# Moving head-norm, value and key-projection steps between the slots of the first two cycles of a fused two-block transformer kernel

## The chip, the cores and the metric

The kernel runs on one core of one Trainium2 chip. The metric is the device time of one execution, in microseconds (us). A core has five engines that take part here: TensorE (PE, matrix multiplication, with a separate record PEld for loading weights), VectorE (DVE), ScalarE (ACT), GpSimd (POOL) and SyncE (SP, which only issues transfers). Each has its own instruction queue and they wait for one another through semaphores.

## The reference, cut to what matters

Two transformer blocks run one after the other over `x` of shape (8, 512, 256): batch 8, 512 tokens, width 256. All data are float32. The first block ("block 0") is the one that the change touches:

```python
mod = silu(c) @ adaln_w.T + adaln_b            # nine rows of 256 per batch element
h = ln(x) * (1 + scale_sa) + shift_sa
q = ln(heads(h)) * qn_w + qn_b                 # 16 heads of 16 columns, each head normed
k = ln(heads(h)) * kn_w + kn_b
x = x + gate_sa * softmax(q k^T / 4) heads(h)  # self-attention, values are h itself
h = ln(x) * (1 + scale_ca) + shift_ca
kv = brain @ cond_w.T + cond_b                 # 64 context tokens of width 192
x = x + gate_ca * (attention(h wq, kv wk, kv wv) @ ca_out_w.T + ca_out_b)
h = ln(x) * (1 + scale_ff) + shift_ff
x = x + gate_ff * ((silu(h w1) * (h w3)) @ w2)
```

The second block has self-attention with 16 heads of 64 columns and rotary position factors, cross-attention to the layer-normed context with rotated keys (`ctx_n @ ca_wk`, computed once for all batch elements), and a GELU feed-forward part.

## The kernel before, in words

Block 0 is one long list of slots. A cycle is 18 slots (`CYCLE = H + 2`), and cycle b holds the 16 score blocks of batch element b: four groups g of four heads, four key tiles kt each, at slots 0 to 17 without 11 and 13 (`X0`, `X1`). In slots 11 and 13 of cycle b + 1 stand the two cross-attention score blocks of element b; in cycle 0 they are empty. Feed-forward of element b runs in cycle b + 2. "Slot n" below counts from the start of the kernel, so cycle 1 is slots 18 to 35.

A score block multiplies four heads at once (PE, tile `ps_S`, L118, 16 rows of each head against 512 query columns), ACT takes the exponential of two halves of 1024 columns (L596, tile `p`), and a value block multiplies `p` by `h` into `ps_O`. There are two `ps_S` tiles and one score block fills both, so the next score block waits for the exponentials of the one before.

All other work is hung on slots by `at(slot, function)`. `run_blocks` walks the slots: in the first 18 it issues the scores of slot i, the values of slot i - 1 and then what `at` hung on slot i; from there on it takes slots in pairs. The order of issue is the order of each engine's queue: the section is recorded under a manual schedule, so nothing is reordered later, and functions on one slot come in the order of their `at` calls. Entries in the list `later` are hung on after everything else.

The steps concerned:

- Head norm of the next element (`batch1`, L640 to L662). After the layer norm and modulation of `h`, the 16 heads are normed in two halves c = 0 and c = 1: `head_centre` (DVE L548 to L550: mean, subtract, into `z`), `head_square` (ACT L554), `head_var` (DVE L560, L561) and `head_scale` (POOL: the power -1/2 at L567 and the product at L568). For element 0 the half c = 0 is split again by parity; `first_modulated` (DVE L535, L536) modulates `h` out of the PSUM tile `first_mod`.
- `queries_keys(g)`: four PE transposes of `z` (L576), then q on ACT (L579) and k on DVE (L580). Group g uses half c = g // 2. For element 1, g = 0 stands in slot 16 and g = 2 in slot 20.
- `group_end` (ACT copy L609) and `group_back(g)`: PE transposes (L616), DVE L623 to L625, then POOL's gating L627 and the addition to `x` L628.
- Set-up of cross-attention: `values0(t)`, t = 0 to 3 (two PE matmuls of 256 columns, four DVE additions L380 into `vb0`), `modulation1` (L391), `modulation1_columns` (PE L396, DVE L397), and the layer-normed context for block 1, turned by `context1(k)` (PE L415, DVE L416).
- Keys of block 1: `keys1(p)`, p = 0 to 7 (two PE matmuls of 512 columns with `w_ck`, DVE L847 and L850 twice, POOL L851) and `store_keys1(p)` (a transfer issued on POOL's queue, L873). `open_cross` at slot 18 closes the set-up pool, and SP then issues the load of `w_ck` into its place (L264).

PSUM tiles for everything else come from `bank_x`: every third is the bank `ps_D`, the others are the two `ps_X` banks. A bank is written again only after its last reader is done.

## Time and profile before

| what | value |
|---|---|
| median of 3 runs (lowest, highest) | 2392.32 us (2385.81, 2396.17) |
| the profiled execution, its own time | 2395.5 us |
| span of that execution on the core | 2393.4 us |
| mean granted TensorE clock | 0.994 |
| PE busy | 2369.5 us, 99% |
| DVE, ACT, POOL busy | 1140.9, 887.8, 960.2 us |

The profiled execution's own time is 2.1 us above its span, which is what lies around the first and last instruction, and 3.2 us above the median. The profile gives times from the span's start. Each group of instructions has its line in the kernel, its engine, the tile it writes and those it reads; `x8` behind four matmuls of float32 is the number of machine instructions. PE's ends are modelled: a score block that stands with 2.04 us instead of 1.14 us has its second half held up, not more work.

The first two cycles reach from 17 us to about 171 us of the span. PE is idle for 3.35 us of the first 60 us, 6.77 us of the second 60 us (53.23 us busy) and 0.84 us of the third. In the second 60 us the granted clock averages 0.83.

### The profile page before, as it was taken

The numbers are of one execution on the slowest core, as the hardware profiler recorded it, in microseconds if no ns is written. First come the engines' busy times: TensorE is split into PE (matmuls) and PEld (weight loads), VectorE is DVE, ScalarE is ACT, GpSimd is POOL, SyncE is SP. The second block draws the span as 40 slices with busy tenths as digits, with TensorE's granted clock in tenths as the row PEclk, the third lists the DMA queues.
The fourth block names the chain that finished last, engine by engine and source line by source line (L and its number), as shares of the span: only waits on it lengthen the run. The fifth ranks groups of instructions, "written<-read, shape, count | busy, mean of one in ns | idle before, by whom it ended". The sixth has DMA issues, their size and how long they took to land.

```text
span 2393.4 us, 28547 instructions
## 1 busy us (share of the span) xinstructions
PE 2369.5 (99%) x10964; PEld 1156.6 (48%) x10964; DVE 1140.9 (48%) x2115; ACT 887.8 (37%) x1118; POOL 960.2 (40%) x588
## 2 busy tenths in 40 slices
PE   9899999999999999999999999999999999999998
PEld 4333544534545633444444444444345566667665
DVE  4464534535335445545455454545444766651110
ACT  4566545555552134333333333333332222221221
POOL 4463323233201037555555555555543545541110
PEclk9899999999999999999999999999999999999999
DMA  5121000000002000000000000000113222210000
GB/s 185 28 88 35 16 13 11 17 16 8 11 14 92 1 1 24 19 19 19 19 19 19 19 19 19 19 19 19 37 56 105 71 68 69 65 57 30 18 23 19
DMA packets 84897, 84.07 MB, mean 35 GB/s; under 512 B 42656, under 2 KB 59792, under 8 KB 84752
## 3 DMA queue, kind: packets, MB, share of 16 engines
q1 hardware_dynamic: 83208, 78.99, 10.6%
q8 instruction: 88, 1.44, 0.2%
q0 software_dynamic: 640, 2.10, 0.2%
q10 hardware_dynamic: 904, 1.07, 0.1%
q14 instruction: 57, 0.47, 0.1%
HBM read 72.09 MB, written 10.04 MB: 34 GB/s over the span
## 4 chain that ended last, share of the span: by engine, by line
PE 94%; DVE 2%; POOL 1%; issue 1%; DMA 1%; ACT 1%; SPq 0%; POOLq 0%; DVEq 0%; ACTq 0%
PE ps_X L118 39%; PE ps_S L118 24%; PE ps_D L118 15%; PE ps_O L118 14%; PE ps_X L429 1%; POOL var L567 1%; DMA rb<-rec 1%; PE ps_X L616 0%; PE ps_X L576 0%; DVE t L850 0%; DMA rec<-rec 0%; PE ps_D L576 0%; PE ps_D L429 0%; PE ps_D L616 0%; ACT p L596 0%
## 5 line engine op out<-in xcount | busy, mean ns | idle before, releaser
L118 PE MATMUL ps_S<-q,k 32*128 32x512 f32 (+1 forms) x3072 | 421.3, 628 | 5.5 <-ACT p L596 3.4
L1027 ACT ACTIVATE p<-ps_S 128x1024 f32<-128x1024 f32 x256 | 248.4, 1021 | 449.4 <-PE ps_S L118 449.1
L596 ACT ACTIVATE p<-ps_S 128x1024 f32<-128x1024 f32 x256 | 248.2, 1022 | 201.3 <-PE ps_S L118 200.4
L118 PEld LDWEIGHTS ps_S<-q,k 32*128 32x128 f32 (+1 forms) x3072 | 143.0, 185 | 231.9 <-issue 162.5
L1046 DVE TENSOR_TENSOR sm<-sm,p 128x1024 f32<-128x1024 f32 x128 | 252.4, 2030 | 0.1
L1009 POOL TENSOR_TENSOR q<-t 128x512 f32<-128x512 f32 x32 | 59.7, 1866 | 331.3 <-DVE t L1007 290.2
L1006 DVE TENSOR_TENSOR t<-ps_X,rope_c 128x512 f32<-128x512 f32 x126 | 86.9, 689 | 213.0 <-PE ps_X L118 213.0
L184 POOL TENSOR_TENSOR rstd<-rstd,mhalf 128x4 f32<-128x4 f32 x49 | 50.1, 1023 | 331.8 <-DVE rstd L183 330.4
L851 POOL TENSOR_TENSOR q<-t,t 128x512 f32<-128x512 f32 x72 | 94.9, 1318 | 159.2 <-DVE t L850 159.2
L567 POOL TENSOR_TENSOR var<-var,mhalf 128x32 f32<-128x32 f32 (+1 forms) x17 | 87.3, 5137 | 159.0 <-DVE var L561 158.9
L1042 POOL TENSOR_TENSOR sm<-p 128x1024 f32<-128x1024 f32 x64 | 150.0, 2370 | 1.9 <-ACT p L1027 1.9
L118 PE MATMUL ps_X<-hT,w 128*128 128x512 f32 x328 | 150.4, 597 | 0.0
L1092 POOL TENSOR_TENSOR oT<-oT,rb 128x512 f32<-128x512 f32 x63 | 126.9, 2032 | 28.8 <-DMA rb<-rec_d 28.8
L118 PE MATMUL ps_O<-p,v 128*64 128x512 f32 x512 | 134.9, 605 | 0.0
L118 PE MATMUL ps_O<-p,h 128*32 128x512 f32 x1024 | 131.6, 618 | 0.6 <-ACT p L596 0.6
L118 PE MATMUL ps_D<-p,v 128*64 128x512 f32 x512 | 131.6, 592 | 0.0
L118 PE MATMUL ps_X<-w_sa_wv,hT 128*128 128x512 f32 x256 | 118.0, 604 | 0.0
L118 PE MATMUL ps_X<-hT,w_sa_wq 128*128 128x512 f32 x256 | 115.9, 595 | 0.0
L118 PE MATMUL ps_X<-w_sa_wo,oT 128*128 128x256 f32 x512 | 113.9, 381 | 0.6 <-DVE t L1007 0.5
L118 PE MATMUL ps_X<-hT,w_sa_wk 128*128 128x512 f32 x248 | 113.2, 599 | 0.0
L466 DVE TENSOR_TENSOR x<-ps_X,x 128x512 f32<-128x512 f32 x27 | 18.7, 691 | 195.6 <-PE ps_X L118 195.6
L118 PE MATMUL ps_S<-hT,w_ff_w 128*128 128x512 f32 x256 | 111.3, 593 | 0.0
(285 smaller groups left out, 3622.0 us busy)
## 6 DMA issues: line engine op xcount, KB each, us to landing
rb<-rec SPq DMA_DIRECT2D x128, 128.0 KB
rb<-rec_d SPq DMA_DIRECT2D x124, 128.0 KB
rb<-rec SPq DMA_DIRECT2D x16, 256.0 KB
out_dram<-x SPq DMA_DIRECT2D x15, 256.0 KB
x<-in_x_dram SPq DMA_DIRECT2D x7, 512.0 KB
gate<-modd SPq DMA_DIRECT2D x24, 128.0 KB
k_d<-q POOLq DMA_DIRECT2D x8, 256.0 KB, 2.4
v_d<-v SPq DMA_DIRECT2D x8, 256.0 KB
```

The source lines that it names most:

```text
L118: nc.tensor.matmul(o, lhsT, rhs, start=start, stop=stop)
L184: nc.gpsimd.tensor_tensor(r[:, :n], r[:, :n], mhalf[:, :n], ALU.pow)
L429: nc.tensor.transpose(ps[:, t * P : (t + 1) * P], z[:, t, k * P : (k + 1) * P], ident)
L567: nc.gpsimd.tensor_tensor(var, var, half, ALU.pow)
L596: nc.scalar.activation(pr[u], pss[u], AF.Exp, scale=HD0 ** -0.5)
L851: nc.gpsimd.tensor_tensor(dst, t1, t2, ALU.add)
L1006: nc.vector.tensor_tensor(c, ps, rope_c, ALU.mult)
L1009: nc.gpsimd.tensor_tensor(r[0], ec, os, ALU.subtract)
L1027: nc.scalar.activation(pr, pss[u], AF.Exp, scale=HD1 ** -0.5)
L1042: nc.gpsimd.tensor_tensor(sm, s["p", g, 0, u], s["p", g, 1, u], ALU.add)
L1046: nc.vector.tensor_tensor(s["sm", g, u], s["sm", g, u], s["p", g, t, u], ALU.add)
L1092: eng.tensor_tensor(o, o, s["rb", g, u], ALU.mult)
```

## The change

Four things move between slots; no instruction is added or taken away.

- Element 1's head norm: its two halves ran together in slots 12 to 14. Now half 0 has its `head_scale` in slot 13 instead of 14, in front of `group_back(2)`'s gating of slot 14 on POOL's queue, and half 1 runs in slots 15 to 17.
- `values0(0..3)` stood in slots 10, 11, 14 and 15 and stands in 14, 15, 16 and 17.
- `keys1(p)` stood in slots 22, 23, 25, 27, 28, 30, 32 and 33 and stands in 20, 22, 24, ... 34. `store_keys1(p)` stood in slots 25, 26, 28, 30, 31, 33, 35 and 36 and stands in 23, 25, 27, 29, 31, 33, 35 and 36.
- Element 0's `first_modulated(1)` stays in slot 2 but goes behind `queries_keys(1)` of that slot, through `later`, whose definition moves up for it.

```diff
@@ batch1
                         for k, par, fns in ((0, 1, (first_modulated, head_centre)),
-                                            (1, 1, (head_square, head_var, head_scale)), (2, None, (first_modulated,)),
+                                            (1, 1, (head_square, head_var, head_scale)),
                                             (3, None, (head_centre,)), (4, None, (head_square, head_var, head_scale))):
                             for fn in fns:
                                 at(k, lambda fn=fn, par=par: fn(0 if par else 1, par))
                         at(5, lambda: spread(s["gate"], b, G_SA, D))
+                        later.append((at, 2, lambda: first_modulated(1)))
                     else:
 
                         for m, k in enumerate((-11, -10, -9) if b == 1 else (-13, -12, -10)):
                             at(i + k, lambda m=m: norm(m))
                         for c in range(2):
-                            for k, fn in zip((-6, -5, -5, -4) if b == 1 else (-7, -5, -3, -3) if c else (-9, -8, -7, -7),
+                            for k, fn in zip(((-6, -5, -5, -5), (-3, -2, -1, -1))[c] if b == 1 else (-7, -5, -3, -3) if c else (-9, -8, -7, -7),
                                              (head_centre, head_square, head_var, head_scale)):
                                 at(i + k, lambda c=c, fn=fn: fn(c))
@@ the slots of set-up
+    later = []
     blocks = [Block([], []) for _ in range(CYCLE * (B + 2))]
...
-    for t, i in enumerate((10, 11, 14, 15)):
+    for t, i in enumerate((14, 15, 16, 17)):
         at(i, lambda t=t: values0(t))
@@ the keys of block 1
     for p in range(NPAIR):
-        at(CYCLE + 4 + 5 * p // 3, lambda p=p: keys1(p))
-        at(CYCLE + 7 + 5 * p // 3, lambda p=p: store_keys1(p))
+        at(CYCLE + 2 + 2 * p, lambda p=p: keys1(p))
+        at(min(CYCLE + 5 + 2 * p, 2 * CYCLE), lambda p=p: store_keys1(p))
...
-    later = []
     for b in range(B):
```

## The prediction

> **What bounds the kernel now.** I read the page's busy times first, then the chain of waits, then PE's timeline over the first two cycles with the clock in 2 us windows. The page says that PE is the engine to watch, and that its clock has one visible hole, in the second of the 40 slices (59.8 us each):

> ```profile
> PE 2369.5 (99%) x10964; PEld 1156.6 (48%) x10964; DVE 1140.9 (48%) x2115; ACT 887.8 (37%) x1118; POOL 960.2 (40%) x588
> PEclk9899999999999999999999999999999999999999
> ```

> So a step moved off PE gains nothing; only PE's idle time and slow clock do. The chain of waits, asked for 57 to 112 us, names what holds PE there (start, length, what):

> ```profile
> 73.92 0.43 DVE attn L625
> ...
> 74.42 0.73 POOL attn L627
> ...
> 75.24 0.72 POOL x L628
> 75.96 5.39 POOL var L567
> ...
> 81.44 1.06 POOL z L568
> ...
> 82.55 1.11 PE ps_D L576 x4
> ```

> The head norm's power (5.4 us) stands in POOL's queue behind the gating of group 2, which needs DVE's L625. PE's transposes of `z` wait for it. PE's timeline (start, length, idle before) has that wait and an earlier one:

> ```profile
> 72.30 2.04 PE L118 MATMUL ps_S<-q,k 16*128 16x512 f32 x8 [2.05 <-ACT p L596]
> ...
> 82.55 1.11 PE L576 MATMUL ps_D<-ident,z 128*128 128x128 f32 x4 [3.08 <-POOL z L568]
> ```

> The 2.05 us: ACT's exponentials of slot 14 start at 71.24, behind two head squares at 69.22 and 70.70 that waited for DVE. And the windows show what the 3.08 us cost beyond themselves (column after POOL: granted clock):

> ```profile
> 80.00:82.00 2.00, 0.00 (x0) 0.00 (x0) 0.00 (x0) 0.50 (x1) 1.92 (x2) 1.00 0.00 0
> 82.00:84.00 2.00, 1.45 (x7) 1.45 (x8) 0.00 (x0) 0.30 (x1) 2.00 (x2) 0.52 0.00 0
> ...
> 100.00:102.00 2.00, 2.00 (x12) 0.44 (x12) 0.00 (x0) 1.13 (x2) 0.00 (x0) 0.50 0.00 0
> 102.00:104.00 2.00, 2.00 (x16) 0.31 (x8) 0.00 (x0) 0.00 (x0) 0.00 (x0) 0.86 0.00 0
> ```

> In tenths of a microsecond the half clock lasts from 82.1 to 102.57, and once more from 167.43 to 170.84.

> [...] 20.47 us is 6.00 windows, 3.41 us is one, and the second drop lies 19 windows after the first ended. [...]

> **The change, part by part**, against the profiled execution's own 2395.5 us (3.2 above the median; 2.1 of it lies around the span). S(n), O(n) are scores and values of slot n; a free S or O takes 1.07 of PE, four transposes 0.5, `values0` 1.06.

> 1. `values0` leaves slots 10 and 11. O(10) no longer starts behind it, but needs the second exponential (58.87 + 1.94 = 60.81) and then 1.0 for its second half: S(12) at 61.9 instead of 62.91. Two steps of 1.06 leave, 1.1 comes back as waiting: **-1.0**. q, k and S(14) follow (67.65 to 66.66).

> 2. Only one head square stands in front of exponential 14. k ends at 66.6, `z` at 68.14 (k start + 2.35, as before), the square runs 68.23 to 68.86, the exponential starts at 68.77 (before: 71.24), S(15) at 69.83 (before: 72.30): another **-1.5**. S(16) comes at 74.85 (before: 77.32), since slots 14 and 15 keep one `values0` each.

> 3. The power. Var is ready at 69.8 (square end, 0.69, 0.18). POOL is free (its L184 ends near 65.4), so 5.43 + 0.08 + 1.06 end at 76.45. PE arrives at 79.46 - 2.47 = 76.99. The 3.08 wait is gone with 0.5 to spare: **-3.1**. The gating of group 2 goes from 74.42 to 76.5; nobody waits for it until the norm of `x` at 107.43.

> 4. `values0(2)` and `(3)` now stand in slots 16 and 17: **+2.1** of PE work, the two steps taken from 10 and 11.

> 5. A new wait. In the built program's order the `context1(0)` transposes (L415) take the `ps_X` bank that `queries_keys(0)` filled, and wait for k; before they took another. ACT: S(16) + 1.23 = 76.08, exponentials 1.83, the second square 0.54, q 0.78 to 79.23; k 0.81 to 80.07. PE is ready at 78.8 (transposes 0.5, `values0` 1.06, L396 0.25 after 76.99): **+1.3**. Queued behind it are S(17) and all PE work. Bounds: 0 if ACT's square overlaps, 2 if k is behind DVE's L380.

> S(17) to S(21): moved head half 1 has POOL done by about 90 and is read near 100. Sum of 1 to 5: -1.0 - 1.5 - 3.1 + 2.1 + 1.3 = **-2.2**.

> 6. The clock. Without the long wait the half clock need not come. Its price is not 10.2: part of that time is waiting for ACT. The same sequence at full clock later (S 178.48, L576, S, O x16, S 184.62) takes 6.14; S, O, L415, S, O in front 4.7 plus 0.3 waiting; together 11.1 from S(17) to S(21), against 84.87 to 103.03 = 18.16. The transposes 82.55 to 84.87 take 2.32 instead of 1.25. **-8.1**.

> 7. Keys. Between S(21) and S(23) PE takes 103.03 to 109.17 = 6.14 for 4.5 of work (two S, L616 0.5, O x16 1.86). `keys1(0)` (1.88) now stands there and covers ACT: **-1.6**. Taken from where two key steps stood together, it uncovers nothing I find. One fewer rope (2.1 on DVE) precedes element 2's variance, so POOL's `z` is in time at 150.85: **-0.5**. `keys1(2)` in `ps_D` now waits for L625, 1.74 after L616 starts, against 1.46 of PE work: **+0.3**. The store issues (0.6 to 0.75 each on POOL) keep their number; the last two stay on slot 36, so SP's feed-forward loads behind them don't move in order. The load of `w_ck` follows PE's last set-up read: 89.91 becomes about 84.3; it and the other transfers issued after it had landed 6.1 later (windows to 96), so 90.4, and `keys1(0)` reads at 94.2. Hidden by the four slots between; without them up to 6.

> 8. `first_modulated(1)` behind k in slot 2: 1.4 later on DVE, `z` at 35.1, covered by exponential 4 on ACT until 36.16. **0**; without that cover 1.4.

> Sum: -2.2 - 8.1 - 1.8 = -12.1: **2383.4**. The second drop (167.43) costs 1.7 [...]; I take half of it away: **2382.5**.

> **Rivals.**
> - *The clock falls anyway.* Weighing PE's work by the rows and columns in use, without transposes, I estimate from the timeline that the windows before the two drops held 0.18 and 0.21 of full use, and no window that kept the clock less than about 0.3 (0.23 in one full of transposes). After the change PE does only transposes and waits from 78.5 to 80.6, and S(19), L576, S(20) at half rate fill 86.4 to 90.7; a window that begins in some 1.9 of the 3.4 us has 0.23 to 0.27. [...] The loss is 4 to 10: **2386 to 2393**.
> - *More than counted*: no drop anywhere, and step 5's wait near 0: **2379**; with run-to-run spread like the before's, down to 2375.
> - *The change does nothing here*: the power is still late, because var is. It would need 0.5 us on the ACT-DVE chain; then 3 returns step by step and so does the clock: **2391 to 2396**.
> - *Slower*: the clock drops at 81.9, at step 5's wait, and no window is dense enough until the long projections near S(27). That is 32.5 us of full-clock work (82 to 114.5) at half clock, of which ACT's waits hide a fifth: +26, **2407**. Before, windows with estimates of 0.67 and 0.58 did not restore the clock, one with 0.90 did. It decides only if all of nine windows stay under that; values and `values0` standing together in slot 17 make a dense one, which speaks against it.

> **How the numbers follow.** Likeliest (0.48): the wait goes and the clock holds or drops for a window, 2379 to 2386. More than counted 0.22; clock falls 0.22; nothing 0.03; slower 0.05. A measurement of this kernel can tell about 0.5% (12 us) from no change, so faster means below 2380.4: all but a little of the second case and four tenths of the first, 0.40. Slower means above 2404.3: 0.05. The rest, 0.55, is the same. The range, 2376 to 2393, leaves out the slower case, the worst of the fallen clock and the lowest runs.

> **What would show it.** Right: L576 of slot 16 with no wait for POOL, the power at about 70 before the gating, clock 1.00 from 80 to 104, a wait of about 1.3 of L415 for k, S(22) not waiting for ACT. Wrong: half clock between 80 and 115, PE waiting for `w_ck`, or `z` still late. Then the clock, not the order, sets the result.

## The result: 0.3 to 0.4% less time

| | kernel before | kernel after |
|---|---|---|
| median (lowest, highest), first comparison, 7 runs each | 2392.35 us (2385.81, 2396.82) | 2384.86 us (2383.23, 2386.47) |
| median (lowest, highest), second comparison, 43 and 22 runs | 2393.04 us (2385.95, 2397.50) | 2384.80 us (2382.05, 2391.24) |
| profiled execution: its time, span, mean clock | 2395.5, 2393.4, 0.994 | 2383.23, 2381.4, 0.999 |

The ratio after to before is 0.9963 (95% interval 0.9952 to 0.9974) in the first comparison and 0.9971 (0.9963 to 0.9979) in the second. The kernel after is faster, by less than the 0.5% of the prediction's bound. The spans of the two profiled executions differ by 12.0 us. That is more than the difference of the medians, 7.5 and 8.2 us, and the experiments show why.

On the page of the kernel after, the busy times of the engines are nearly as before (PE has 8.8 us less), and the hole in the clock's digits is gone:

```profile
PE 2360.7 (99%) x10964; PEld 1152.7 (48%) x10964; DVE 1139.6 (48%) x2115; ACT 886.9 (37%) x1118; POOL 959.5 (40%) x588
PEclk9999999999999999999999999999999999999999
```

POOL's timeline of the kernel after (start, length, line, out<-in, idle before) shows the moved head norm:

```profile
69.21 5.49 POOL L567 TENSOR_TENSOR var<-var,mhalf 128x32 f32<-128x32 f32 x1 [4.52 <-DVE var L561]
74.78 1.06 POOL L568 TENSOR_TENSOR z<-z,var 128x512 f32<-128x512 f32 x1
75.80 0.73 POOL L627 TENSOR_TENSOR attn<-attn,gate 128x256 f32<-128x256 f32 x1
```

The power now runs at 69.21 instead of 75.96, ahead of the gating of L627. PE's timeline of the kernel after has the consequences (same columns):

```profile
61.26 1.14 PE L118 MATMUL ps_S<-q,k 16*128 16x512 f32 x8
...
69.17 2.04 PE L118 MATMUL ps_S<-q,k 16*128 16x512 f32 x8 [0.57 <-ACT p L596]
...
76.26 0.66 PE L576 MATMUL ps_X<-ident,z 128*128 128x128 f32 x4
...
79.45 0.64 PE L415 MATMUL ps_X<-ident,ctx_z 128*96 128x128 f32 x4 [1.45 <-DVE k L580]
...
85.90 2.04 PE L118 MATMUL ps_S<-q,k 16*128 16x512 f32 x8 [0.17 <-ACT p L596]
87.88 0.66 PE L576 MATMUL ps_X<-ident,z 128*128 128x128 f32 x4
88.46 2.13 PE L118 MATMUL ps_S<-q,k 16*128 16x512 f32 x8
90.52 3.23 PE L118 MATMUL ps_O<-p,h 128*32 128x512 f32 x16
...
95.25 1.88 PE L118 MATMUL ps_D<-ctxzT,w_ck 96*128 96x512 f32 x4
97.06 1.14 PE L118 MATMUL ps_S<-q,k 16*128 16x512 f32 x8
```

From top to bottom these are S(12), S(15), the transposes of slot 16 without a wait, the new wait of L415, then S(19), transposes, S(20) and the two value blocks, `keys1(0)` and S(22) without a wait for ACT. Up to L415 all of it lies 0.6 us earlier than the prediction's times. That offset is no effect of the change: the first wait for k ends at 18.91 us here and at 19.49 us before, ahead of every moved step, and the three kernels below in which one part moves alone have it too (18.84 to 18.99).

The chain of waits of the kernel after (start, length, what) passes, where POOL stood before, through ACT and DVE to the wait of L415:

```profile
77.37 0.52 ACT ln L554
77.88 0.68 ACT q L579
...
78.59 0.82 DVE k L580
```

The windows of the kernel after (window, length, busy time of PE, PEld, DVE, ACT and POOL, granted clock, DMA share, GB/s):

```profile
78.00:80.00 2.00, 0.55 (x5) 0.39 (x4) 1.39 (x4) 0.55 (x1) 0.00 (x0) 1.00 0.00 0
80.00:82.00 2.00, 2.00 (x17) 0.47 (x16) 1.92 (x5) 0.74 (x1) 0.00 (x0) 1.00 0.00 0
...
88.00:90.00 2.00, 2.00 (x12) 0.89 (x12) 0.00 (x0) 2.00 (x4) 1.06 (x1) 0.95 0.86 212
90.00:92.00 2.00, 2.00 (x10) 0.40 (x12) 0.81 (x1) 2.00 (x3) 0.00 (x0) 0.50 0.03 8
92.00:94.00 2.00, 2.00 (x16) 0.51 (x12) 0.00 (x0) 0.06 (x1) 0.00 (x0) 0.70 0.00 0
```

The clock is full at 80 to 88, where it was half before, although PE stood idle from 78.0 to 79.45. It is half for one window of 3.41 us, 89.80 to 93.21, in which PE was never idle. So the waits went as forecast. Of the 12.0 us between the two profiles 0.6 are the offset and the waits and work were forecast at 4.0, so most of it is the clock (granted 0.994 before and 0.999 after). The question for the chip was what the clock answers to.

### The profile page after: what moved, and what is told of

The parts are those of the page before. It is cut to its first block, busy times and chain, and to the rows that moved or that the text cites. A ratio compares the mean times of both kernels' runs of the same rounds, so it can differ in the third digit from the quotient of the medians.

```text
span 2381.4 us, 28545 instructions
## 1 busy us (share of the span) xinstructions
PE 2360.7 (99%) x10964; PEld 1152.7 (48%) x10964; DVE 1139.6 (48%) x2115; ACT 886.9 (37%) x1118; POOL 959.5 (40%) x588
## 3 DMA queue, kind: packets, MB, share of 16 engines
q10 hardware_dynamic: 904, 1.07, 0.2%
## 4 chain that ended last, share of the span: by engine, by line
PE 96%; DVE 1%; DMA 1%; ACT 1%; issue 1%; POOL 0%; SPq 0%; ACTq 0%; POOLq 0%; DVEq 0%
PE ps_X L118 39%; PE ps_S L118 24%; PE ps_D L118 16%; PE ps_O L118 14%; PE ps_X L429 1%; PE ps_X L616 1%; DMA rb<-rec 0%; PE ps_X L576 0%; ACT p L596 0%; DVE t L852 0%; PE ps_D L616 0%; PE ps_D L429 0%; POOL var L567 0%; DMA rec<-rec 0%; PE ps_D L576 0%
## 5 line engine op out<-in xcount | busy, mean ns | idle before, releaser
L118 PE MATMUL ps_S<-q,k 32*128 32x512 f32 (+1 forms) x3072 | 417.4, 622 | 3.7 <-ACT p L596 1.5
L596 ACT ACTIVATE p<-ps_S 128x1024 f32<-128x1024 f32 x256 | 248.2, 1022 | 195.9 <-PE ps_S L118 195.2
L118 PEld LDWEIGHTS ps_S<-q,k 32*128 32x128 f32 (+1 forms) x3072 | 141.8, 183 | 229.6 <-issue 160.6
L184 POOL TENSOR_TENSOR rstd<-rstd,mhalf 128x4 f32<-128x4 f32 x49 | 50.2, 1024 | 329.7 <-DVE rstd L183 328.4
L567 POOL TENSOR_TENSOR var<-var,mhalf 128x32 f32<-128x32 f32 (+1 forms) x17 | 87.4, 5140 | 168.1 <-DVE var L561 168.0
L118 PE MATMUL ps_X<-hT,w 128*128 128x512 f32 x328 | 150.6, 597 | 0.2 <-DVE t L788 0.2
L118 PE MATMUL ps_O<-p,v 128*64 128x512 f32 x512 | 134.9, 605 | 0.0
L118 PE MATMUL ps_D<-p,v 128*64 128x512 f32 x512 | 131.6, 592 | 0.0
L118 PE MATMUL ps_O<-p,h 128*32 128x512 f32 x1024 | 129.3, 605 | 0.8 <-ACT p L596 0.8
L118 PE MATMUL ps_X<-w_sa_wv,hT 128*128 128x512 f32 x256 | 118.0, 604 | 0.0
L118 PE MATMUL ps_X<-hT,w_sa_wq 128*128 128x512 f32 x256 | 115.9, 595 | 0.0
L118 PE MATMUL ps_X<-w_sa_wo,oT 128*128 128x256 f32 x512 | 113.9, 381 | 0.6 <-DVE t L1008 0.5
L118 PE MATMUL ps_X<-hT,w_sa_wk 128*128 128x512 f32 x248 | 113.2, 599 | 0.0
L118 PE MATMUL ps_S<-hT,w_ff_w 128*128 128x512 f32 x256 | 111.3, 592 | 0.0
```

Source lines behind the costliest of these rows:

```text
L118: nc.tensor.matmul(o, lhsT, rhs, start=start, stop=stop)
L184: nc.gpsimd.tensor_tensor(r[:, :n], r[:, :n], mhalf[:, :n], ALU.pow)
L567: nc.gpsimd.tensor_tensor(var, var, half, ALU.pow)
L596: nc.scalar.activation(pr[u], pss[u], AF.Exp, scale=HD0 ** -0.5)
```

## The experiments

"The theory" of the first four runs is the prediction's: the 3 us in which PE stood still before the transposes of slot 16 cost the half clock behind it. All medians, in us, each beside the kernel before on the same chip. Three chips were used; the median of the kernel before on them was 2393.27, 2392.15 and 2393.04, so two changed kernels that ran on different chips compare less closely than each does with the kernel before. The column "half clock" gives the stretches of that kernel's profiled execution up to 300 us. The column "clock loss" is the mean over all runs of the time that the clock withheld, (1 - granted clock) times the span, in us; the kernel before loses 10.0, 9.8 and 10.2 on the three chips. The standard error of such a mean is 0.4 to 0.9 us, for the narrow filling 1.8:

| kernel | median (lowest, highest) | runs | difference of medians | ratio, 95% interval | half clock | clock loss |
|---|---|---|---|---|---|---|
| head norm alone | 2388.17 (2382.49, 2392.82) | 17 | -5.1 | 0.9967 to 0.9989 | 72.6-76.0, 89.6-93.0, 96.5-103.3, 175.0-178.4 | 8.3 |
| wait filled, wide | 2395.37 (2388.84, 2398.64) | 13 | +2.1 | 0.9999 to 1.0022 | 73.8-77.2, 94.3-97.7, 101.1-118.2, 169.4-172.8 | 10.7 |
| wait filled, narrow | 2394.27 (2389.22, 2402.37) | 14 | +1.0 | 1.0001 to 1.0031 | 75.0-78.4, 160.3-163.7 | 12.5 |
| after, old head norm | 2387.17 (2385.39, 2393.19) | 21 | -6.1 | 0.9968 to 0.9983 | 73.2-76.6, 93.6-97.1 | 5.6 |
| keys alone | 2386.40 (2382.91, 2391.83) | 22 | -5.8 | 0.9967 to 0.9983 | 74.2-77.6 | 6.2 |
| values alone | 2389.28 (2387.06, 2395.05) | 14 | -2.9 | 0.9980 to 1.0003 | 70.8-77.7, 159.6-163.0 | 7.3 |
| after, old values | 2382.35 (2379.84, 2387.11) | 8 | -9.8 | 0.9945 to 0.9975 | 89.4-92.8, 154.2-164.5 | 4.5 |
| after, late context | 2384.01 (2380.22, 2387.86) | 17 | -8.1 | 0.9960 to 0.9980 | none | 5.5 |
| old values, single 19 | 2381.63 (2380.36, 2382.42) | 6 | -11.4 | 0.9945 to 0.9976 | 72.7-76.1, 168.2-171.6 | 2.8 |
| old values, single 36 | 2386.54 (2382.64, 2391.17) | 22 | -6.5 | 0.9969 to 0.9985 | none | 3.9 |
| after again | 2384.80 (2382.05, 2391.24) | 22 | -8.2 | 0.9963 to 0.9979 | 71.4-74.8, 91.9-95.3 | 5.6 |

The time follows the granted clock: over the runs of one kernel (13 or more) the correlation of time and clock loss is 0.85 to 0.97. Taken as the clock's cost the loss is an estimate from above, since half clock that stands beside a wait costs less than it withholds: the half clock from 82.1 us in the kernel before withheld 10.2 us, and the work from the transposes of slot 16 to S(21) took 20.48 us there against 12.65 at full clock in the run of keys alone, 7.8 more.

**Head norm alone.**

```diff
-  zip((-6, -5, -5, -4) if b == 1 else ...
+  zip(((-6, -5, -5, -5), (-3, -2, -1, -1))[c] if b == 1 else ...
```

> The kernel before with the head-norm step alone moved (half 0 scaled in slot 13, half 1 in slots 15 to 17). Theory (the wait for POOL's z and the half clock behind it carry the gain): exponential 14 comes 1.5 us sooner, the transposes of slot 16 (L576) start without a wait (-3.1 us), no wait of L415 for k arises because the value steps are where they were and L415 has another bank, and the half clock from 82 to 102.6 does not come, or comes for one 3.4 us window. The step alone is then worth as much as the whole change: 2381 to 2386 us, ratio to before 0.996 to 0.998. Rival (the other moves carry it, or the clock drops whatever this wait does): only the 4.6 us of waits go, hidden in part by the exponentials at half clock, and the half clock stays for several windows: 2388 to 2392 us.

Its median is 5.1 us below before, at the lower edge of the rival's range. Its profile settles more. The transposes start without a wait at 78.85, so the moved step did all that it should, and the half clock still comes four times, in five windows, three of them between 89 and 104 us. Taking the wait away doesn't keep the clock: over its 17 runs the clock loss is 8.3 us against 10.0.

**The wait filled with matmuls.** The matmuls stand ahead of the transposes in the tile that these overwrite:

```diff
@@ queries_keys
+            for _ in range(7 if b == 1 and g == 0 else 0):
+                mm(ps[:, 0:256], ident, chk.rearrange("p i c -> p (i c)"))
             for t in range(NT):
                 nc.tensor.transpose(...)
```

> The kernel before, in its own order, with seven full-size matmuls of 256 columns (0.44 us each, 3.1 us in all, results overwritten) ahead of the slot-16 transposes, in the place where PE stood waiting for POOL's z. The wait is filled, not removed: the transposes still start at about 82.5 us. Theory (the half clock was caused by the empty 3.1 us): the clock stays at 1.00 from 82 to 102, S(21) comes some 8 us sooner, 2384 to 2387 us. Rival (the narrow score work and transposes drop the clock with or without the wait): clock 0.5 for several windows after 82, time as before or up to 1 us over, 2391 to 2394 us.

PE's timeline of this kernel shows the idle time filled (L578 is what L576 was), and its windows show the clock full just behind it and half 18 us later, for 17 us:

```profile
80.27 3.29 PE L118 MATMUL ps_D<-chk,ident 128*128 128x256 f32 x14
83.39 0.60 PE L578 MATMUL ps_D<-ident,z 128*128 128x128 f32 x4
```

```profile
82.00:84.00 2.00, 2.00 (x14) 1.77 (x13) 0.00 (x0) 0.00 (x0) 2.00 (x1) 1.00 0.00 0
...
102.00:104.00 2.00, 2.00 (x10) 0.40 (x12) 1.93 (x9) 1.24 (x2) 0.00 (x1) 0.50 0.21 66
```

PE arrived 0.8 us later than at 79.47, behind the window at 73.8 to 77.2 at half clock, in which `values0` took 2.08 us (1.13 in the kernel before). POOL's `z` was ready at 81.76, so the filling overshot by 1.6 us in this execution, and that is what the filling itself cost there. The median came out 2.1 us above before, where the theory wanted 2384 to 2387 us, and the clock loss, 10.7 us, is no smaller than before. With that the theory falls: if the empty 3 us were what costs the time, full-size work in their place would have brought it back.

**The same with narrow matmuls.**

```diff
+                mm(ps[0:32, 0:256], ident[0:16, 0:32], chk[0:16].rearrange("p i c -> p (i c)"))
```

> As the run with seven full-size matmuls in the wait, but with seven that use 16 rows and 32 columns of the array, of the same 256 columns of data and so the same time. PE is as busy in the record as in that run. Theory (what the clock goes by is how much of the array is in use, as my estimate of 0.18 to 0.21 against 0.29 and more assumed): the clock falls at about 82 as before, 2390 to 2394 us. Rival (it goes by whether PE is busy at all): clock 1.00 as in the full-size run, 2384 to 2387 us.

The narrow filling takes 3.20 us and the wide one 3.29, and PE is busy for all of the time from 80 to 84 us in both. 2394.27 us is about what the use-of-the-array theory said, but the wide filling's time is the same within its interval. Since neither filling brought time back, the pair can't tell wide from narrow: inconclusive for what it was built for. Five of the 14 narrow runs took 2401.2 us or more, at clocks of 0.991 to 0.993, and none of the 13 wide ones went beyond 2398.64; that leans towards the use-of-the-array theory, and is too little to show it. Its profile has the window that is hardest for that theory, told below.

**The kernel after with the old head norm.** The edit is made in the kernel after:

```diff
-  zip(((-6, -5, -5, -5), (-3, -2, -1, -1))[c] if b == 1 else ...
+  zip((-6, -5, -5, -4) if b == 1 else ...
```

> The kernel after with the head norm of element 1 put back (both halves in slots 12 to 14), all other moves kept. Theory: the wait of L576 for POOL is back at about 3 to 4 us, the half clock of about 20 us with it, and the two value steps that now stand in slots 16 and 17 and the wait of L415 for k run at half clock too: 2391 to 2397 us, at or above the kernel before. Rival (the value and key moves are what saves the time): 2384 to 2388 us.

2387.17 us, 6.1 below before: the theory is refuted from the other side. The wait is back, and the clock is full behind it (PE's timeline, then the windows). Over all runs the clock loss is 5.6 us, as in the kernel after with the moved head norm:

```profile
80.80 0.66 PE L576 MATMUL ps_X<-ident,z 128*128 128x128 f32 x4 [1.50 <-POOL z L568]
...
83.17 0.64 PE L415 MATMUL ps_X<-ident,ctx_z 128*96 128x128 f32 x4 [0.63 <-DVE k L580]
```

```profile
80.00:82.00 2.00, 1.20 (x8) 1.13 (x9) 0.00 (x0) 0.84 (x2) 2.00 (x2) 1.00 0.00 0
82.00:84.00 2.00, 1.37 (x12) 0.88 (x14) 1.66 (x5) 0.27 (x1) 2.00 (x1) 1.00 0.00 0
```

The wait is 1.5 here and not 3, behind a half-clock window at 73.2 that withheld 1.7 us. The run of keys alone, told below, has the order of before up to there, and has the same: half clock from 74.2 to 77.6, PE ready at 80.51 instead of 79.47 (1.6 us later with the 0.6 of offset), and a wait of 1.51 instead of 3.08. So the half clock hides some of its own cost in waits.

**A second theory.** In each trace all changes of the clock lie on one grid of 3.4133 us (in the profile of before they lie 20.48, 64.85 and 3.41 us apart: 6, 19 and 1 times that). Its place in the span differs from run to run: the remainder of those times by 3.4133 is 0.18 in the profile of before, 1.05 in that of after, and between 0.6 and 3.3 in the others. So the same order of work is cut into windows of 3.41 us at another place each time, and a stretch that falls whole into one window in one run is split over two in the next. To see what the windows answer to, I took, for each whole window of each trace from 16 to 300 us, the sum over its matmuls, transposes left out, of time in the window times rows / 128 times columns / 128 (the largest matmuls of the traces stand with 128*128), divided by 3.4133 (the records of successive matmuls overlap, so it can pass 1). It is called the use of the array here. With all 13 traces:

| clock in the window, and in the next | windows | this use of the array | PE busy |
|---|---|---|---|
| half, then full | 24 | 0.96 to 1.34 | 1.00 |
| half, then half | 13 | 0.09 to 0.87 | 0.87 to 1.00 |
| full, then half | 24 | 0.25 to 0.61, 18 of them at most 0.34 | 0.23 to 1.00 |
| full, then full | 1007 | 10 of them at most 0.34, 122 at most 0.61 | 0.53 to 1.00 |

In these traces the clock comes back after windows with a use of 0.96 or more, and after no other: PE was busy all of the time in 12 of the 13 windows that left it half. It goes after windows with a use of 0.25 to 0.61, whether PE waits in them or not: PE was busy all of the time in 6 of the 24. Not every window of so little use loses it. The ten exceptions at most 0.34 are all windows in which the transposes, left out of the sum, take 0.72 or more of a window by the same measure; in the 24 that lost the clock they take at most 0.34. The window at 81.81 in the narrow filling held 0.03 of other use and 0.72 of transposes, and kept the clock. So in these traces transposes count for something in keeping the clock. That is a fit to traces, not a test, and between 0.35 and 0.61 it doesn't separate. (By this sum the windows before the two drops of the kernel before held 0.27 and 0.33, those that left it half 0.09 to 0.86 and those that restored it 1.02 and 1.08; the prediction's estimates of 0.18 and 0.21, of 0.67 and 0.58, and of 0.90 were read from merged lines.)

**Keys alone.**

```diff
-        at(CYCLE + 4 + 5 * p // 3, lambda p=p: keys1(p))
-        at(CYCLE + 7 + 5 * p // 3, lambda p=p: store_keys1(p))
+        at(CYCLE + 2 + 2 * p, lambda p=p: keys1(p))
+        at(min(CYCLE + 5 + 2 * p, 2 * CYCLE), lambda p=p: store_keys1(p))
```

> The kernel before with the keys1 and store_keys1 slots alone moved. My sum gave this step -1.6 (keys1(0) fills the stretch from S(21) to S(23) where PE waited for ACT), -0.5 and +0.3: -1.8 in work and waits. The earlier theory of the clock (the wait for POOL's z brings the half clock) fell with the filled waits, so the present theory is that the chip's windows of 3.41 us fall anywhere on this stretch, and that the clock is halved after a window in which little of the array was in use, whatever the cause, and restored after one that uses nearly all. keys1(0) is dense work right behind the score blocks S(19) to S(21): besides the -1.8 some long drops should end sooner. Present theory: 2388 to 2391 us. Rival (only the work and waits count): 2391.5. Second rival (the step is hidden behind ACT anyway): 2393.

2386.40 us: 5.8 below before, more than any of the three answers. The head norm is the old one here, POOL's wait is there, and the clock stays full from 77.6 to 2381 us (PE's timeline: the wait, then S(17), S(20), O x16 and S(21); the window behind it). That is one draw: its 22 runs have clocks of 0.995 to 0.999. But their mean loss is 6.2 us against 9.8, so this step does help to hold the clock:

```profile
82.02 0.66 PE L576 MATMUL ps_D<-ident,z 128*128 128x128 f32 x4 [1.51 <-POOL z L568]
...
83.26 1.14 PE L118 MATMUL ps_S<-q,k 16*128 16x512 f32 x8
...
90.85 2.04 PE L118 MATMUL ps_S<-q,k 16*128 16x512 f32 x8
92.82 1.92 PE L118 MATMUL ps_O<-p,h 128*32 128x512 f32 x16
94.67 1.20 PE L118 MATMUL ps_S<-q,k 16*128 16x512 f32 x8
```

```profile
82.00:84.00 2.00, 1.98 (x18) 1.38 (x18) 0.48 (x1) 0.78 (x1) 2.00 (x1) 1.00 0.00 0
```

This profile also measures what the prediction's step 6 priced. S(17) to S(21) takes 94.67 - 83.26 = 11.41 us at full clock, against 18.16 in the profile of before; the prediction had 11.1.

**Values alone.**

```diff
-    for t, i in enumerate((10, 11, 14, 15)):
+    for t, i in enumerate((14, 15, 16, 17)):
```

> The kernel before with the four values0 steps alone moved (slots 14 to 17). By my sum of work and waits this step alone makes the kernel slower: -1.0 from slots 10 and 11, +2.1 in slots 16 and 17, +0.6 for L415 waiting for k, together +1.7: 2395 us is what the rival (only work and waits count) says. Present theory: two full-array steps stand now in the stretch from the transposes of slot 16 to S(18), where windows with little of the array in use halved the clock, so the long half clock from 82 to 102 becomes rarer and the kernel is not slower, 2388 to 2392 us, although the wait for POOL's z stays.

2389.28 us, with an interval that reaches from 0.2% faster to no change. It isn't 2395, so work and waits alone don't give its time: the clock loss is 7.3 us against 9.8. If all of that is taken off the means, 0.0 is left of their difference, where the sum said a loss of 1.7; no run shows why.

**The kernel after with the old values.** The edit is made in the kernel after:

```diff
-    for t, i in enumerate((14, 15, 16, 17)):
+    for t, i in enumerate((10, 11, 14, 15)):
```

> The kernel after with values0 put back in slots 10, 11, 14 and 15. In work and waits that is +1.0, -2.1 and -1.45 (L415 has its other bank again and doesn't wait for k): -2.5, which alone would give 2382.3 us and beat the kernel after. Rival and present theory of the clock: without the two full-array steps in slots 16 and 17 windows between 80 and 100 us halve the clock more often, as in the run with the head norm alone (three drops), which gives back 0 to 4 us: 2383 to 2386 us with a wider spread of its runs than the kernel after (3.2 us).

2382.35 us: what work and waits alone give, 2.5 below the kernel after. L415 doesn't wait in its trace. The spread of its runs, 7.3 us, is the other answer's, though the 3.2 us that this was set against did not last (below). There are only eight runs, on another chip, and the interval doesn't part it from the kernel after.

**The kernel after with a later context step.**

```diff
-    at(16, lambda: context1(0))
+    at(17, lambda: context1(0))
```

> The kernel after with context1(0) moved from slot 16 to slot 17, behind S(17), O(16) and values0(3). The wait of L415 for k (1.45 us) goes; values0(3) is what takes the bank of queries_keys(0) then, 2 us later, when k is done. Theory (the wait is a loss on PE's path): -1.4, 2383.4 us, S(18) 1.4 us sooner. Rival (ACT's exponentials set the pace of slots 17 to 20 and swallow it): 2384.9 as the kernel after, with a wait of S(18) or S(19) for ACT in its place.

The median moved by -0.8 against the kernel after (2384.80, on another chip), which the intervals don't part. In the trace the wait is gone and nothing takes its place (PE's timeline: S(16), S(17), S(18)):

```profile
74.36 1.14 PE L118 MATMUL ps_S<-q,k 16*128 16x512 f32 x8
...
78.10 1.14 PE L118 MATMUL ps_S<-q,k 16*128 16x512 f32 x8
...
82.10 1.14 PE L118 MATMUL ps_S<-q,k 16*128 16x512 f32 x8
```

S(17) starts 3.74 us after S(16) instead of 5.84, of which the moved transposes are 0.5. S(18) comes 7.74 us after S(16) instead of 9.40, and S(19) waits 0.17 for ACT as in the kernel after. The wait was a real loss: the mean time less the clock loss, each against the kernel before, is -4.1 us here and -2.6 in the kernel after, an estimated 1.5 apart. It is smaller than what the clock adds or takes between runs. The profiled execution has no half-clock window before 2377 us: 2378.8 us of span is what this order takes at full clock. That, too, is one draw: seven of its 17 runs have a clock of 0.996. The single window of the kernel after's profile cost 1.6 us: S(17) to S(21) takes 13.65 there and 12.45 here, where 0.44 of it is the moved step.

**Breaking the stretch.** If a row of score blocks and transposes is what drops the clock, putting the value blocks between them should keep it. The first kernel has the old values and walks slots 19 and 20 one at a time:

```diff
-    run_blocks(blocks, beside, behind, CYCLE)
+    run_blocks(blocks, beside, behind, CYCLE + 2)
```

> The kernel after with values0 back in slots 10, 11, 14 and 15, and slots 19 and 20 walked one at a time like the first 18, so that O(18) stands between S(19) and S(20) and the transposes of slot 18 before S(19). Theory (the half clock follows windows that use little of the array, and S(19), transposes, S(20) in a row are such a stretch whatever waits there are): no half-clock window that begins between 86 and 94 us, so about 1.6 us less in the runs that had one: median 2380.5 to 2382 us, against 2382.35 for the version with the pair. Rival (the drop near 90 has another cause, or the pair was there for ACT's sake and its waits come instead): 2383 to 2385 us.

PE's timeline of it, S(18) to S(20) with a value block behind each score block:

```profile
82.69 1.71 PE L118 MATMUL ps_S<-q,k 16*128 16x512 f32 x8
84.33 1.06 PE L118 MATMUL ps_O<-p,h 128*32 128x512 f32 x8
85.33 0.66 PE L576 MATMUL ps_X<-ident,z 128*128 128x128 f32 x4
85.92 1.14 PE L118 MATMUL ps_S<-q,k 16*128 16x512 f32 x8
86.99 1.07 PE L118 MATMUL ps_O<-p,h 128*32 128x512 f32 x8
87.99 0.66 PE L616 MATMUL ps_X<-ident,oT 128*128 128x128 f32 x4
88.57 1.70 PE L118 MATMUL ps_S<-q,k 16*128 16x512 f32 x8
```

As expected there is no half clock between 76.1 and 168.2, and the median is 2381.63 us. All of its six runs, 2380.36 to 2382.42, lie below 21 of the 22 of the kernel after on the same chip. It has the lowest median and the smallest clock loss (2.8 us) of all, and is faster than both kernels, though its ratio's interval and that of the kernel after (0.9945 to 0.9976, 0.9963 to 0.9979) overlap. How much of that the broken pair gives, and how much the old values, is not shown: the kernel with the pair and the old values (2382.35, eight runs on another chip) has a run below all six of these, and a clock loss of 4.5 us, larger by 1.7 with a standard error of 0.8.

The second, also with the old values, walks all slots to 36 one at a time:

```diff
-    run_blocks(blocks, beside, behind, CYCLE)
+    run_blocks(blocks, beside, behind, 2 * CYCLE)
```

> As the run with slots 19 and 20 walked one at a time, but all slots to 36, which also breaks the pair of score blocks near 157 us, where five of the runs so far show a half clock. Theory: no drop between 80 and 180 us, 2379 to 2382 us, spread of the runs below 5 us. Rival: walked one at a time every slot waits for ACT (0.58 us a time in slots 12 to 15 of the kernel after), 18 slots lose 5 to 10 us: 2387 to 2392 us.

In the profiled execution the clock is as the theory said, with no half-clock window before 2381 us. The other runs say less: seven of the 22 have a clock of 0.997, and the mean loss, 3.9 us, is not clearly below the 4.5 of the kernel with the pairs. The time isn't as the theory said: 2386.54 us, spread 8.5 us. Its span of 2382.9 without a drop is 4.1 above that of the late-context kernel without one, and its median 4.2 above that of the kernel with the old values and all pairs: the pairs do serve to hide ACT, and undoing them costs more than the clock gives back. Of the 4.1 us PE's timelines show 2.4 at the 24 score blocks from S(19) on: they wait for ACT 1.32 us and stand 7.62 us beyond 1.14 us each in this kernel, 0.77 and 5.76 in the late-context kernel. The rival's 2387 to 2392 lies just above the median.

**The kernel after again.**

> The kernel after itself, beside the two variants on the same chip, for its spread over more runs. If the chip's windows fall at a random phase, its runs lie between about 2381.6 us (no half-clock window: 2383.23 less the 1.6 us that the one window of its profile cost) and some 2388 us (two or three windows), median 2384 to 2386 us. Rival (its profile, one window at 89.8, is what always happens): all runs within 2383 to 2386.5 us.

Its 22 runs lie between 2382.05 and 2391.24 us, four of them above the 2388 that was expected as the most; the seven runs of the first comparison had shown a third of that range. The profile has two half-clock windows, one of them in slots 14 and 15, where the one at 89.8 was the only one of the first profile. So one order of work can give different windows. The spread goes with the clock: the correlation of time and clock loss is 0.89, the run at 0.995 took 2391.24 us and the four at 0.999 took 2382.05 to 2384.88. That the clock differs because the grid lies elsewhere is my guess and not shown: the place of the grid is known only in the profiled runs. Fourteen of the 22 lie within the range of the first seven, so seven in a row there have a chance of 4%: the first spread was luck, unless the chip had a part in it.

## Why the prediction was right, and where it was not

The 2382.5 us forecast are 2.4 us under the 2384.86 measured, inside the range, and the gain stays within the 0.5% to which the forecast gave 0.55. Step by step (times less the 0.6 us of offset):

1. Values out of slots 10 and 11: S(12) forecast at 61.3, seen at 61.26. Right.
2. One head square ahead of the exponential: S(15) forecast at 69.2, seen at 69.17, its wait for ACT down from 2.05 to 0.57. Right.
3. The power: variance forecast at 69.2, seen at 69.21; `z` done at 75.84, forecast 75.9; no wait left. Right, and the 0.5 us of margin came out at 0.4.
4. and 5. The two values in slots 16 and 17 and the new wait of L415, forecast 1.3, seen 1.45. Right. That the wait is a real loss is shown by the late-context run's trace.
6. The clock, -8.1. The price was right (11.1 forecast for S(17) to S(21), 11.41 measured at full clock). **The cause was wrong**, and this is the step that failed: "Without the long wait the half clock need not come" took one profiled execution's six half-clock windows as the kernel's own. The wait can be filled without gain, and it can stay without a half clock behind it; with the old head norm back in the kernel after, the clock loss is 5.6 us, as without it. What the profile of before showed was one draw, with a clock of 0.994 where its runs reach from 0.992 to 0.998. The proper term is a difference between two distributions: the mean clock loss falls from 10.2 to 5.6 us, 4.6 and not 8.1.
7. Keys: S(22) doesn't wait for ACT, `keys1(2)` waits 0.23 for L625 (0.3 forecast), element 2's transposes find `z` in time, `w_ck` was issued at 83.73 and nobody waited for it. Right in its waits; it missed that the same step helps to hold the clock (loss 6.2 against 9.8 us when it moves alone).
8. `first_modulated(1)`: the wait behind it is 1.30 before and after. Zero, right.

Of the signs that the prediction named, one of those for "wrong" came too: the clock was not full from 80 to 104 us but half from 89.8 to 93.2.

That the number came out well is in part luck. The mean time falls by 7.2 us (2392.67 to 2385.50, second comparison) and the mean clock loss by 4.6, with a standard error of 0.7; counted in full, that leaves 2.6 for work and waits. The forecast had 4.0 for work and waits and 9.0 for the clock (8.1 and the 0.9 of the second drop, half of its 1.7, which was my estimate): about twice what the clock gave. But it started from a profiled execution that was 3.2 us above the median and whose clock lost about 14 us, where the mean of 43 runs is 10.2. A start that was too high and a gain that was too large cancel in part. The lowest runs of the two kernels differ by 3.9 us, like the forecast sum without the clock, but they don't show it: at clocks of 0.998 and 0.999 they lost about 4.8 and 2.4 us, so that of the kernel before at least is not free of half clock ahead of its last microseconds (1.9 us in its profile).

The three parts alone add up to -13.7 in the medians, against -8.2 together. Their clock losses fall by 7.8 us in sum, against 4.6 together: more than half of the gap is half clock that can be saved only once.

Of the rivals, "the clock falls anyway" named the place (S(19), L576, S(20)) where the kernel after loses its window in both profiles; it gave that case too large a price, 4 to 10 us, since the clock came back after one window in both profiles, with the two value blocks (L118, `x16`), whose windows use 1.00 and 1.08 of the array by the sum above. "More than counted" is what the late-context run reached in its profile. The slower case, a half clock that stays for many windows, was not seen in the kernel after; the longest in any of the changed kernels' profiles was that of the wide filling (101.1 to 118.2). Its 2407 is 26 above 2381, where the forecast of 2382.5 gives 2408.5; nothing else hangs on that sum.

What stays open: what parts the windows that lose the clock from those that keep it between 0.35 and 0.61 of use, how much a transpose counts, why the mean leaves 2.6 us for work and waits where each step of the timeline came out as forecast and they sum to 4.0, and where the half-clock windows fall in runs without a profile, of which only the mean clock is recorded.

## What to carry to other kernels

A half clock in one profile of a kernel with narrow matmuls can be a draw and not a property (0.992 to 0.998 over the runs of the kernel before): before pricing it, look at the spread of the runs and at the granted clock of each, and treat the price as a change of chances. What lowered the clock loss here was dense work moved right behind rows of score blocks and transposes (the key projections alone: 3.6 us less, standard error 0.8); the removal of the wait gave 1.7 alone, with an error of 1.0, and nothing on top of the other moves. Count the waits apart from the clock: in the timeline they came out within 0.2 us of their forecasts, one by one, and the clock's share didn't.
